# Reordering the last stage of a gated cross-attention and mixture-of-experts kernel: the last expert's down product, the routed rows' additions, and the last store

## The chip, the cores and the metric

One core of one Trainium2 chip runs the whole kernel. The metric is device time in microseconds of one execution, as a median of runs. Five engines matter: PE (TensorE, matrix products), DVE (VectorE), ACT (ScalarE), POOL (GpSimd) and SP (SyncE, which here only issues DMAs). PEld is the weight load that goes with each matmul.

## The reference

Four batches of 512 tokens with 512 features pass two layers. The first, per batch, is a quantised gated product with weights of its own. The second is a mixture of experts over all 2048 tokens, and the change lies in it:

```python
x = x + tanh(g_xattn[0]) * quantised_glu(layernorm(x), fside, ctx)
h = layernorm(x).reshape(-1, 512)                      # 2048 tokens
topk_w, topk_idx = top_k(softmax(h @ gate_w.T), 2)     # 16 experts, 2 per token
buf[e, pos] = h[token]                                 # 256 places per expert
expert_out = einsum(silu(buf @ w_gate) * (buf @ w_up), w_down)     # inner width 352
y = sum over the 2 experts of topk_w * expert_out[expert, pos]     # back to tokens
sh = (silu(h @ ws_gate) * (h @ ws_up)) @ ws_down       # shared expert, width 704
x = x + tanh(g_ffn[0]) * (y + sh)
```

All of it is float32.

## The kernel before

The residual `X` stays in SBUF as 16 tiles `X[:, j, :]` of 128 tokens by 512 features. Tiles 0 to 11 (batches 0 to 2) get their shared expert earlier; tiles 12 to 15 (batch 3) get it at the end of the kernel, after the routed experts.

*Routed experts.* A loop over `e` runs 16 experts of 256 token places, two halves `h` of 128. `gate_up(e)` computes the gate and up products (L1138) and writes the features to two tiles `home.h[h]` (named `h_e` in the profile; L1205 and L1213). `turn_features(e)` transposes both on TensorE (L1158, `tp_h`), six transposes. `join_features(e, h)` copies a transposed half from PSUM to `ehT` on VectorE (L1165). `down_routed(e)` makes the two down products into PSUM tiles `eo` (L974), of three chunks of the inner width each. `take_down(e, h)` copies one to SBUF on ScalarE (L1149) and stores it to the DRAM tensor `eo_dram` from ScalarE's own queue (L1150). The down product of an expert follows the gate and up product of the next one. For the last expert there is no next one: before the change, the gate product of chunk 0 of the shared expert stands between the turning of its features and its down.

*The end.* The shared expert of batch 3 has five full chunks of 128 of its inner width and a rest of 64. `chunk_steps(c)` gives for a chunk: four gate products (`pg`, L959), the silu on ScalarE (L963), four up products (`pu`, L959), and the product of both on VectorE (`times`, L966), which writes `hT`. The rest has one product `pr` for gate and up together (L998), its silu (L1002) and two products on VectorE (L1010). Then, for tiles `t` = 0 to 3 in two pairs `u`, `tokens_product` (L1024) and `rest_tokens` (L1030) multiply `hT` by the down weights into PSUM `sh`, and `tokens_add` (L1034) adds it to `X` and calls `store`, a DMA issued by SP (L1635).

*Routed rows.* `gather_result` (L1659) gathers on POOL, for one tile and one of its two experts, 128 rows of `eo_dram` by `slot` into a tile `yk`; there are 32 gathers and 20 buffers, and a gather beyond the 20th is issued after the addition that frees its buffer. `add_results(upto)` (L1670) adds rows to `X` on VectorE until `upto` of the 32 are done, in the order tiles 12 to 15, then 0 to 11, two rows a tile; the second addition of a tile below 12 is followed by its store. The gathers begin after `routed.close()`, which gives back the buffers of the routed experts, of which the buffers `yk` take the place.

*Order.* Everything here stands under `tc.manual_schedule()`: each engine runs its instructions in the order in which the program text emits them, and semaphores put the engines in step. The order of the last stage is written out by hand, and the tuples in the text say how far `add_results` goes at each place. PSUM has rings of buffers: `ps_t` (2, transposes), `ps_c` (2, down products) and `ps_mm` (4, tag `mm`: gate, up, rest and token products, taken in turn).

Of the kernel before, what the change touches and what calls it, by code (L numbers as in the profile page):

```python
# [9 lines left out]
F32 = mybir.dt.float32  # L10
# [5 lines left out]
ALU = mybir.AluOpType  # L16
# [4 lines left out]
P = 128  # L21
B, S, H = 4, 512, 512
HC = H // P
TT = S // P
NT = B * TT
# [3 lines left out]
E = 16  # L29
CAP = 256  # L30
# [6 lines left out]
CHUNKS_I = [(0, 128), (128, 128), (256, 96)]  # L37
CHUNKS_IS = [(c * P, min(P, IS - c * P)) for c in range((IS + P - 1) // P)]
FULL = IS // P
# [81 lines left out]
def flamingo_gated_kernel(  # L121
# [16 lines left out]
    nc = tc.nc  # L138
    vec, act, pe, pool = nc.vector, nc.scalar, nc.tensor, nc.gpsimd
# [5 lines left out]
    ps_c = ctx.enter_context(tc.tile_pool(name="ps_c", bufs=2, space=PSUM))  # L145
# [13 lines left out]
    X = const.tile([P, NT, H], F32, tag="X", name="X")  # L159
    x_flat = x.rearrange("b (t p) h -> p (b t) h", p=P)  # L160
    out_flat = out.rearrange("b (t p) h -> p (b t) h", p=P)
# [53 lines left out]
    tg_f = const.tile([P, 1], F32, tag="tg_f", name="tg_f")  # L215
# [756 lines left out]
    def down(acc, hT, t, wd, chunks):  # L972
        for c, (_, m) in enumerate(chunks):
            pe.matmul(  # L974
                acc, lhsT=hT[:m, c, bass.ts(t, P)], rhs=wd[:m, c, :], start=(c == 0), stop=(c == len(chunks) - 1)
            )

    def shared(b, done=None):
        s = SimpleNamespace()

        def chunk_steps(c, home=(shp, 2)):
            if c == 0:
                s.hT = shp.tile([P, len(CHUNKS_IS), S], F32, tag="hT", name="hT")
            return glu_steps(xTs[b], c * P, s.hT[:, c, :], home)

        def chunk(c):
            gate, silu, up, times = chunk_steps(c)
            for step in gate + up:
                step()
            silu()  # L990
            times()

        def rest_product(k):


            if k == 0:
                s.pr = ps_mm.tile([P, H], F32, tag="mm", name="pr")
            pe.matmul(s.pr, lhsT=wsr[:, k, :], rhs=xTs[b][:, k, :], start=(k == 0), stop=(k == HC - 1))  # L998

        def rest_silu():  # L1000
            s.g = shp.tile([P, S], F32, tag="g", name="g_rest", bufs=2)
            act.activation(s.g[:REST], s.pr[:REST], AF.Silu)  # L1002

        def rest_times(odd):

            gate, up, dst = (
                a.rearrange("p (u v q) -> p u v q", v=2, q=P)[:, :, odd]
                for a in (s.g[:REST], s.pr[REST:], s.hT[REST * odd : REST * (odd + 1), FULL, :])
            )
            vec.tensor_tensor(dst, gate, up, ALU.mult)  # L1010

        def rest():
            for k in range(HC):
                rest_product(k)
            rest_silu()
            rest_times(0)
            rest_times(1)

        accs = {}

        def tokens_product(t, c, last):
            if c == 0:
                accs[t] = ps_mm.tile([P, H], F32, tag="mm", name="sh")
            pe.matmul(accs[t], lhsT=s.hT[:, c, bass.ts(t, P)], rhs=wsd[:, c, :], start=(c == 0), stop=(c == last))  # L1024

        def rest_tokens(u, last):

            for odd in range(2):
                t, rows = 2 * u + odd, slice(REST * odd, REST * (odd + 1))
                pe.matmul(accs[t], lhsT=s.hT[rows, FULL, bass.ts(t, P)], rhs=wsd[rows, FULL, :], start=False, stop=last)  # L1030

        def tokens_add(t):
            j = b * TT + t
            vec.scalar_tensor_tensor(X[:, j, :], accs[t], tg_f, X[:, j, :], ALU.mult, ALU.add)  # L1034
            if done is not None:
                done(j)

        s.__dict__.update({k: f for k, f in locals().items() if callable(f)})

        s.chunk_steps = chunk_steps  # L1040
        s.all = [lambda c=c: chunk(c) for c in range(FULL)] + [rest]
        return s
# [7 lines left out]
    R = [SimpleNamespace(xg={}) for _ in range(E)]  # L1050
    HALF = HC // 2

    E_W = {e: {} for e in range(E)}
# [93 lines left out]
    def take_down(e, h):  # L1147
        eo = qb.tile([P, H], F32, tag="h", name="eo_sb", bufs=3)
        act.copy(eo, R[e].acc[h])  # L1149
        nc.scalar.dma_start(out=eo_dram[e * CAP + h * P : e * CAP + (h + 1) * P, :], in_=eo)  # L1150

    def turn_features(e):
        r = R[e]
        r.tps = []
        for h in range(CAP // P):
            tp = ps_t.tile([P, HC, P], F32, tag="tp", name="tp_h")
            for c in range(len(CHUNKS_I)):
                pe.transpose(tp[:, c, :], home.h[h][:, bass.ts(c, P)], ident)  # L1158
            r.tps.append(tp)

    def join_features(e, h):
        r = R[e]
        if h == 0:
            r.hT = qb.tile([P, len(CHUNKS_I), CAP], F32, tag="wc", name="ehT", bufs=2)
        vec.tensor_copy(r.hT[:, :, bass.ts(h, P)], r.tps[h][:, : len(CHUNKS_I), :])  # L1165

    def gate_up(e):
# [46 lines left out]
        if more:  # L1214
            for step in combine_tokens(e + 1):
                step()

    def down_routed(e):
        r = R[e]
        r.acc = {}  # L1220
        for h in range(CAP // P):
            r.acc[h] = ps_c.tile([P, H], F32, tag="c", name="eo")
            down(r.acc[h], r.hT, h, E_W[e]["down"], CHUNKS_I)
        take_down(e, 0)
        if e + 2 < E:
            load_down(e + 2)
# [392 lines left out]
    with tc.manual_schedule():  # L1619
        plan.run()  # L1620
        open_features()
        for e in range(E):
            gate_up(e)
            if e > 0:
                down_routed(e - 1)
            turn_features(e)
            if e == 1:
                routing_weights(qb)

    def store(j):
        nc.sync.dma_start(out=out_flat[:, j, :], in_=X[:, j, :])  # L1635

    sh3 = shared(B - 1, store)

    tiles = list(range(NT - TT, NT)) + list(range(NT - TT))
    with tc.manual_schedule():  # L1640
        chunks = [sh3.chunk_steps(0)]
        take_down(E - 2, 1)
        for step in chunks[0][0] + [chunks[0][1]]:
            step()
        for h in range(CAP // P):
            join_features(E - 1, h)
        down_routed(E - 1)
        take_down(E - 1, 1)
        for step in chunks[0][2] + [chunks[0][3]]:
            step()  # L1650
        routed.close()
        homes = 20
        results = ctx.enter_context(tc.tile_pool(name="results", bufs=homes))
        yks = []

        def gather_result():
            i = len(yks)
            yk = results.tile([P, H], F32, tag="yk", name="yk")
            pool.indirect_dma_start(  # L1659
                out=yk,  # L1660
                out_offset=None,
                in_=eo_dram,
                in_offset=bass.IndirectOffsetOnAxis(ap=slot[i % 2][:, tiles[i // 2] : tiles[i // 2] + 1], axis=0),
            )
            yks.append(yk)

        def add_results(upto):
            while added[0] < upto:
                j, k = tiles[added[0] // 2], added[0] % 2
                vec.scalar_tensor_tensor(  # L1670
                    X[:, j, :], yks[added[0]], wk[k][:, j : j + 1], X[:, j, :], ALU.mult, ALU.add
                )
                if k == 1 and j < NT - TT:
                    store(j)
                added[0] += 1
                if len(yks) < 2 * NT:
                    gather_result()

        added = [0]
        for i in range(homes):  # L1680
            gather_result()
        for c in range(1, FULL):
            chunks.append(sh3.chunk_steps(c, (results, 4)))
            for step in chunks[c][0] + [chunks[c][1]]:
                step()
        for k in range(HC):
            sh3.rest_product(k)
        sh3.rest_silu()
        for c, upto in zip(range(1, FULL), (7, 9, 12, 15)):
            for step in chunks[c][2]:  # L1690
                step()
            add_results(upto)
            chunks[c][3]()
            if c == 2:
                sh3.rest_times(0)
                sh3.rest_times(1)

        for u, uptos in enumerate(((22, 23), (27, 2 * NT))):
            for t in (2 * u, 2 * u + 1):
                for c in range(FULL - 1):  # L1700
                    sh3.tokens_product(t, c, FULL - 1)
            sh3.rest_tokens(u, False)
            for t, upto in zip((2 * u, 2 * u + 1), uptos):
                sh3.tokens_product(t, FULL - 1, FULL - 1)
                add_results(upto)
                sh3.tokens_add(t)
# [41 lines left out]
```

## Time and profile before

| | |
|---|---|
| median of 3 runs | 585.71 us (585.59 to 585.83) |
| the profiled execution's own time | 585.57 us |
| its span | 583.5 us |
| PE busy | 529.3 us (91%) |
| DVE busy | 405.1 us (69%) |
| ACT busy | 228.9 us (39%) |
| POOL busy | 138.2 us (24%) |
| last stage, chunk 0 of the shared expert to the end | 513.1 to 583.5 us |

Times in the profile count from the start of the span. A row of the timeline gives start, length, engine, line, operation, output and inputs, count, and in brackets how long the engine had been idle and which work ended that. A row of the windows gives, for a stretch, the busy time and number of instructions of each engine, TensorE's granted clock (1.00 is full speed), the mean busy share of the 16 DMA engines and what they moved.

### The profile page before, as it was taken

How to read it: one execution, taken by the hardware profiler on the slowest of the kernel's cores; microseconds unless marked ns; L12 is line 12 of the kernel's file. 1: busy time of each engine (PE TensorE's matmuls, PEld its weight loads, DVE VectorE, ACT ScalarE, POOL GpSimd, SP SyncE). 2: the span in 40 equal slices, each digit the busy share in tenths (PEclk: the TensorE clock that was granted, in tenths of full speed). 3: DMA queues.
4: the chain of work that ended last, by engine and by line, in shares of the span. 5: the costliest groups of instructions: out<-in, count | busy, mean ns of one | idle time of the engine just before them, and what ended most of it. 6: DMA issues, size and time to landing. Idle time of an engine off the chain costs nothing.

```text
span 583.5 us, 5816 instructions
## 1 busy us (share of the span) xinstructions
PE 529.3 (91%) x1760; PEld 275.0 (47%) x1764; DVE 405.1 (69%) x926; ACT 228.9 (39%) x380; POOL 138.2 (24%) x152
## 2 busy tenths in 40 slices
PE   0375499999999999999989999999999999999994
PEld 0232345444444444454455555555555555544441
DVE  3878778998999898987278666666666666304474
ACT  3465366646824272050135434434435343211000
POOL 1212130344143421100310111111212110007770
PEclk9995699999999999999999999999999999999999
DMA  8971012011402365010587999999999995215695
GB/s 295 359 229 38 0 54 92 0 38 54 91 1 54 56 232 155 20 72 1 131 209 223 264 249 269 276 236 276 262 260 274 276 276 173 87 72 160 200 319 187
DMA packets 93774, 95.05 MB, mean 163 GB/s; under 512 B 51488, under 2 KB 69920, under 8 KB 93744
## 3 DMA queue, kind: packets, MB, share of 16 engines
q1 hardware_dynamic: 84016, 69.52, 44.5%
q0 software_dynamic: 5120, 16.78, 9.2%
q10 hardware_dynamic: 4608, 8.39, 3.8%
q8 instruction: 14, 0.23, 0.2%
q14 instruction: 16, 0.13, 0.1%
HBM read 66.36 MB, written 16.78 MB: 142 GB/s over the span
## 4 chain that ended last, share of the span: by engine, by line
PE 79%; DVE 4%; issue 2%; POOL 1%; ACT 0%; DVEq 0%; POOLq 0%
PE b L1138 22%; PE eo L974 14%; PE pu L959 11%; PE pg L959 11%; PE sh L1024 9%; PE pr L998 2%; PE tp_h L1158 2%; PE acc L565 2%; PE sh L1030 1%; PE rowb L304 1%; PE acc L713 1%; DVE amw_w L414 1%; PE tp_am L296 1%; PE tp_x L760 1%; PE tp_q L358 1%
## 5 line engine op out<-in xcount | busy, mean ns | idle before, releaser
L974 PE MATMUL eo<-wd,ehT 128*128 128x512 f32 (+1 forms) x192 | 85.1, 592 | 0.0
L1089 POOL DMA_INDIRECT xg<-xn_dram,slot_token x32 | 34.8, 1088 | 195.7 <-DMA xp<-xg 161.0
L959 PE MATMUL pg<-xT,wsg 128*128 128x512 f32 x160 | 75.7, 603 | 0.0
L959 PE MATMUL pu<-xT,wsu 128*128 128x512 f32 x160 | 74.0, 595 | 0.0
L1024 PE MATMUL sh<-wsd,hT 128*128 128x512 f32 x160 | 73.9, 597 | 0.0
L974 PEld LDWEIGHTS eo<-wd,ehT 128*128 128x128 f32 (+1 forms) x192 | 36.4, 190 | 42.1 <-issue 37.7
L351 ACT COPY xgT<-xp 128x1024 int16<-128x1024 int16 x31 | 39.5, 1339 | 26.4 <-DMA xp<-xg 26.3
L1187 DVE TENSOR_TENSOR p<-p,b 128x352 f32<-128x352 f32 x16 | 8.3, 521 | 58.8 <-PE b L1138 58.8
L1659 POOL DMA_INDIRECT yk<-eo_dram,slot x32 | 33.5, 1048 | 55.7 <-PE pu L959 46.3
L959 PEld LDWEIGHTS pu<-xT,wsu 128*128 128x128 f32 x160 | 29.3, 190 | 31.2 <-issue 31.1
L1024 PEld LDWEIGHTS sh<-wsd,hT 128*128 128x128 f32 x160 | 28.9, 190 | 31.4 <-issue 30.4
L959 PEld LDWEIGHTS pg<-xT,wsg 128*128 128x128 f32 x160 | 29.0, 193 | 30.3 <-issue 29.5
L1138 PE MATMUL b<-T,S 128*128 128x352 f32 x128 | 40.6, 460 | 0.7 <-DVE S L1129 0.7
L1138 PE MATMUL b<-wg,xgT 128*128 128x352 f32 x128 | 40.6, 460 | 0.0
L1138 PE MATMUL b<-wu,S 128*128 128x352 f32 x128 | 40.5, 459 | 0.0
L1149 ACT COPY eo_sb<-eo 128x512 f32<-128x512 f32 x32 | 18.7, 585 | 47.5 <-PE eo L974 43.5
L1138 PEld LDWEIGHTS b<-T,S 128*128 128x128 f32 x128 | 24.2, 190 | 14.5 <-issue 1.2
L1138 PEld LDWEIGHTS b<-wu,S 128*128 128x128 f32 x128 | 24.3, 190 | 13.5
L490 POOL TENSOR_TENSOR wi<-wi,s_row 128x512 f32<-128x512 f32 x15 | 18.6, 1274 | 46.8 <-ACT s_row L475 46.8
L966 DVE TENSOR_TENSOR hT<-g,pu 128x512 f32<-128x512 f32 x20 | 13.6, 682 | 22.6 <-PE pu L959 22.2
L963 ACT ACTIVATE g<-pg 128x512 f32<-128x512 f32 x20 | 11.9, 596 | 41.9 <-PE pg L959 35.6
L1670 DVE SCALAR_TENSOR_TENSOR X<-yk,wk,X 128x512 f32<-128x512 f32 x32 | 23.1, 748 | 7.4 <-DMA yk<-eo_dram,slot 7.1
(219 smaller groups left out, 857.5 us busy)
## 6 DMA issues: line engine op xcount, KB each, us to landing
wg<-in_L_ffn_w_gate_dram SPq DMA_DIRECT2D x16, 704.0 KB, 5.0
wu<-in_L_ffn_w_up_dram SPq DMA_DIRECT2D x16, 704.0 KB, 6.2
wd<-in_L_ffn_w_down_dram SPq DMA_DIRECT2D x16, 512.0 KB, 5.8
eo_dram<-eo_sb ACTq DMA_DIRECT2D x32, 256.0 KB, 4.7
X<-in_x_dram SPq DMA_DIRECT2D x16, 256.0 KB, 8.3
wi<-in_fside_BxS2xS_dram SPq DMA_DIRECT2D x4, 1024.0 KB, 7.1
xn_dram<-yp SPq DMA_DIRECT2D x16, 256.0 KB, 2.0
out_dram<-X SPq DMA_DIRECT2D x16, 256.0 KB, 4.2
```

The source lines that it names most:

```text
L351: return (vec.tensor_copy if on is vec else act.copy)(dst, src)
L490: on.tensor_tensor(w.wi[:, t, :], w.wi[:, t, :], v.s_row, ALU.mult)
L959: pe.matmul(v.ps[name], lhsT=w[:, k, o : o + P], rhs=xT[:, k, :], start=(k == 0), stop=(k == HC - 1))
L963: act.activation(v.g, v.ps["pg"], AF.Silu)
L966: vec.tensor_tensor(dst, v.g, v.ps["pu"], ALU.mult)
L974: pe.matmul(acc, lhsT=hT[:m, c, bass.ts(t, P)], rhs=wd[:m, c, :], start=(c == 0), stop=(c == len(chunks) - 1))
L1024: pe.matmul(accs[t], lhsT=s.hT[:, c, bass.ts(t, P)], rhs=wsd[:, c, :], start=(c == 0), stop=(c == last))
L1089: pool.indirect_dma_start(out=xg.rearrange("p l n -> p (l n)"), out_offset=None, in_=xn_dram, in_offset=bass.IndirectOffsetOnAxis(ap=slot_ ...
L1138: pe.matmul(ps[:, :I], lhsT=lhs[:, k, :], rhs=rhs[:, k, :], start=(first and k == 0), stop=(k == HALF - 1), skip_group_check=not first,)
L1149: act.copy(eo, R[e].acc[h])
L1659: pool.indirect_dma_start(out=yk, out_offset=None, in_=eo_dram, in_offset=bass.IndirectOffsetOnAxis(ap=slot[i % 2][:, tiles[i // 2] : tile ...
L1670: vec.scalar_tensor_tensor(X[:, j, :], yks[added[0]], wk[k][:, j : j + 1], X[:, j, :], ALU.mult, ALU.add)
```

## The change

Four edits, all in the last stage:

- `down_routed` is split into `down_tile(e, h)` for one half. The loop over experts ends with expert 14; expert 15's gate and up product is followed by the first half of expert 14's down, the turning of expert 15's features, the second half of 14's down, and then both halves of 15's down. All of chunk 0 of the shared expert comes after that.
- The places up to which rows are added change from 7, 9, 12, 15 (at the up products of chunks 1 to 4) to 12, 15, 18, 21.
- The places at the four token tiles change from 22, 23, 27, 32 to 28, 28, 32, 32.
- For the last tile, `tokens_add` works in two halves of 256 columns; the first is stored from SP's queue and the second from ScalarE's.

```diff
         def tokens_add(t):
             j = b * TT + t
-            vec.scalar_tensor_tensor(X[:, j, :], accs[t], tg_f, X[:, j, :], ALU.mult, ALU.add)
-            if done is not None:
-                done(j)
+            last = done is not None and t == TT - 1
+            for cs, on in ((slice(0, H // 2), nc.sync), (slice(H // 2, H), nc.scalar)) if last else ((slice(0, H), nc.sync),):
+                vec.scalar_tensor_tensor(X[:, j, cs], accs[t][:, cs], tg_f, X[:, j, cs], ALU.mult, ALU.add)
+                if done is not None:
+                    done(j, cs, on)
...
+    def down_tile(e, h):
+        r = R[e]
+        if h == 0:
+            r.acc = {}
+        r.acc[h] = ps_c.tile([P, H], F32, tag="c", name="eo")
+        down(r.acc[h], r.hT, h, E_W[e]["down"], CHUNKS_I)
+
     def down_routed(e):
-        r = R[e]
-        r.acc = {}
         for h in range(CAP // P):
-            r.acc[h] = ps_c.tile([P, H], F32, tag="c", name="eo")
-            down(r.acc[h], r.hT, h, E_W[e]["down"], CHUNKS_I)
+            down_tile(e, h)
         take_down(e, 0)
...
-        for e in range(E):
+        for e in range(E - 1):
             gate_up(e)
...
+        gate_up(E - 1)
+        down_tile(E - 2, 0)
+        turn_features(E - 1)
+        down_tile(E - 2, 1)
+        for h in range(CAP // P):
+            take_down(E - 2, h)
+            join_features(E - 1, h)
+        for h in range(CAP // P):
+            down_tile(E - 1, h)
+            take_down(E - 1, h)
...
-    def store(j):
-        nc.sync.dma_start(out=out_flat[:, j, :], in_=X[:, j, :])
+    def store(j, cs=slice(0, H), on=nc.sync):
+        on.dma_start(out=out_flat[:, j, cs], in_=X[:, j, cs])
...
         chunks = [sh3.chunk_steps(0)]
-        take_down(E - 2, 1)
-        for step in chunks[0][0] + [chunks[0][1]]:
-            step()
-        for h in range(CAP // P):
-            join_features(E - 1, h)
-        down_routed(E - 1)
-        take_down(E - 1, 1)
-        for step in chunks[0][2] + [chunks[0][3]]:
+        for step in chunks[0][0] + [chunks[0][1]] + chunks[0][2] + [chunks[0][3]]:
             step()
...
-        for c, upto in zip(range(1, FULL), (7, 9, 12, 15)):
+        for c, upto in zip(range(1, FULL), (12, 15, 18, 21)):
...
-        for u, uptos in enumerate(((22, 23), (27, 2 * NT))):
+        for u, uptos in enumerate(((28, 28), (2 * NT, 2 * NT))):
```

## The prediction

> **What bounds the kernel now.** I read the end of the span first, in four views: windows by stage, the chain of waits, the timeline of VectorE, and the gathers' own page. The windows (stretch, length, then busy time of each engine, granted clock, DMA share):
>
> ```profile
> core 0: us, PE busy (x) PEld busy (x) DVE busy (x) ACT busy (x) POOL busy (x), PEclk, DMA share, GB/s
> 507.00:513.10 6.10, 6.10 (x19) 2.96 (x19) 1.04 (x3) 1.39 (x3) 0.00 (x0) 1.00 0.11 43
> 513.10:516.60 3.50, 3.50 (x11) 1.65 (x10) 1.02 (x2) 0.25 (x1) 0.00 (x0) 1.00 0.20 75
> ...
> 556.10:564.20 8.10, 8.10 (x22) 3.19 (x20) 5.69 (x9) 0.00 (x0) 6.27 (x7) 1.00 0.95 311
> 564.20:575.17 10.97, 10.97 (x29) 4.66 (x28) 4.81 (x7) 0.00 (x0) 3.76 (x4) 1.00 0.78 275
> 575.17:580.17 5.00, 0.82 (x2) 0.00 (x0) 4.90 (x7) 0.00 (x0) 0.00 (x0) 1.00 0.42 157
> 580.17:583.50 3.33, 0.00 (x0) 0.00 (x0) 0.00 (x0) 0.00 (x0) 0.00 (x0) 0.58 0.42 157
> ```
>
> TensorE is busy without a gap at granted clock 1.00 until 575.2; after that its last two matmul instructions remain and VectorE works alone for five microseconds. The chain of waits names the same hand-over (start, length, what):
>
> ```profile
> 573.02 1.06 PE sh L1030 x4
> 574.08 1.07 PE sh L1024 x2
> ...
> 575.84 1.41 DVE X L1670 x2
> ```
>
> What VectorE does there, by its timeline:
>
> ```profile
> 565.33 0.75 DVE L1034 SCALAR_TENSOR_TENSOR X<-sh,tg_f,X 128x512 f32<-128x512 f32 x1 [3.28 <-PE sh L1024]
> ...
> 567.32 2.85 DVE L1670 SCALAR_TENSOR_TENSOR X<-yk,wk,X 128x512 f32<-128x512 f32 x4
> 575.17 0.75 DVE L1034 SCALAR_TENSOR_TENSOR X<-sh,tg_f,X 128x512 f32<-128x512 f32 x1 [5.00 <-PE sh L1024]
> 575.84 3.64 DVE L1670 SCALAR_TENSOR_TENSOR X<-yk,wk,X 128x512 f32<-128x512 f32 x5
> 579.40 0.74 DVE L1034 SCALAR_TENSOR_TENSOR X<-sh,tg_f,X 128x512 f32<-128x512 f32 x1
> ```
>
> Five routed-row additions (L1670) stand after the shared addition of tile 14 and hold back that of tile 15. VectorE had been idle 5.00 us just before. The wait is one of order, not of work, provided the five rows had landed. The gathers:
>
> ```profile
> L1659 POOL DMA_INDIRECT yk<-eo_dram,slot x32: 942/950/1421, 525.9 to 567.9; - x32
> ...
> DMA to landing us min/median/max: 3.4/3.9/6.0
> ```
>
> The 32nd gather starts at 567.86 and the DMA page of 568 to 584 gives it 5.4 us to landing: 573.3. So it was there before TensorE ended, and all 32 additions can be over by then.
>
> **The change, part by part.**
>
> *Down of expert 15 ahead of chunk 0.* No instruction is added. TensorE's order from 507.4 is now 6 down matmuls, 6 transposes, 6 down, then down 15 (12), pg (8), pu (8), in place of 12, 6, pg, 12, pu. By the chain these are 5.16 + 0.66 + 3.44 + 5.16 + 3.43 us in either order, so chunk 0 still ends at 525.4: no change, if nothing runs dry. What may: (a) The transposes now start near 510.0; they need the second `h_e`, done at 508.10 + 0.53 = 508.63. Slack 1.4. (b) Before, pg covered the two copies to `ehT` (L1165). They ended at 514.12, 1.55 after the first transpose at 512.57; now 511.55. Down 15 starts when the second down half ends, 513.4. Slack 1.85; without that cover, each microsecond of lateness is one of TensorE. (c) `ps_c` has two buffers: down 15's first half needs ACT's copy of down 14's first half, 510.2 + 0.59 = 510.8, against 513.4; its second half needs 514.2 against 516.0. (d) The four `eo_dram` stores stay on ACT's queue, 0.33 us of issue each, spaced 2.6 us; the last moves from 522.63 to about 519.4, and the silu of chunk 0 behind it is needed only at 525.4. SP has nothing here.
>
> The gathers on POOL wait for the last of these stores, or for chunk 0: the trace puts the first one's wait down to `PE pu L959`. It starts at 525.89, 0.4 us after pu's last matmul but 1.26 us after the store's landing (522.63 + 2.0). So I take pu, which doesn't move: 525.89. At the other end they start 3.4 us earlier. That would only add slack below.
>
> *Additions placed anew.* Still 32, of 0.75 us. Before, 7 / 9 / 12 / 15 were done by the products of chunks 1 to 4, then 22, 23, 27, 32; now 12 / 15 / 18 / 21, then 28, 28, 32, 32. VectorE is in order, so each product now queues behind more additions, which wait for gathers. POOL issues one each 1.25 us alone and 1.35 to 1.54 beside additions (its timeline, 529.6 to 539.7). Additions 0 to 6 ran at 529.29 to 537.79, 1.42 apart and 3.75 after their gather. So: addition 11 at 529.29 + 11 x 1.42 = 544.9, over at 545.7; chunk 1's product was released at 546.12, 0.4 later. Addition 14 (gather 544.67) lands at 548.4, or at 550.0 if it takes the 5.3 us that gathers took once stores ran (555 to 565): done 549.2 to 550.7; chunk 2's product and the two rest products (0.69 + 0.86) then end at 551.1 to 552.3. TensorE needs them at 542.41 + 3 x 3.43 = 552.7, since the ring of four `mm` banks gives pr's bank to pu of chunk 4. This is the tightest point: slack 0.4 to 1.6, and I cost it at nothing. Chunks 3 and 4 are needed at 558.7 and 564.2 and come by 556 and 559. Addition 27 (gather 562.38 + 5) ends at 568.2, so tiles 12 and 13 get their shared addition at 568 to 569.5 and not 565.3 to 567.4; no one waits for those banks. Additions 28 to 31 follow, the last when gather 31 has landed: 573.3, over at 574.05. Slack to 575.17: 1.1.
>
> SP's stores follow the additions: the first at about 543 in place of 551.94. Until 573 some 14 stores, in place of 11, share the DMA with the gathers, but in 540:550 its share was 0.69 to 0.71, room for about four. A gather later by up to 1.1 us costs nothing.
>
> Here a rule speaks against the change. Beside additions a gather took up to 1.42 us against 0.94. The Trainium skill (GPSIMD Engine Reference, Specifications) says GpSimd shares its SBUF interfaces with VectorE and contends with instructions that have two SBUF inputs; L1670 has two. By it, the five additions that ran after the last gather now all run beside one: 5 x 0.2 = 1.0 us later. By the row, POOL had 0.3 us between gathers and was beside additions for most of them already, so some of that only changes place. By the rule the last addition ends at 575.05, by the row at 574.05; both lie before 575.17, so the sum is the same, but the rule eats the slack, and I keep its end for the range.
>
> *The end.* TensorE's last two matmuls end at 574.01 + 1.98 = 575.99. Tile 14's addition runs 575.17 to 575.92, so tile 15's starts at 576.02. Unsplit it would end at 576.77 in place of 580.14: **-3.37 us**.
>
> *Last store in halves.* One addition of 0.75 becomes two of 256 columns. TENSOR_TENSOR rows give 0.42 (256) and 0.69 (512), so 0.27 less: 0.48 each, the second about 0.4 after the first; over at 576.02 + 0.40 + 0.48 = 576.9, **+0.1**. The store issued at 580.17 was followed by the end 3.33 later. The last two stores moved 512 KB in 1.6 us of DMA time, so half a store saves up to 0.4; and SP need not issue (0.33) both. A second rule weighs here: the Trainium skill (DMA: Bandwidth & Descriptors, Issuing engines are not separate DMA queues) says that two queues save only issue time, as all run on the same 16 engines. By the row alone -0.4; by the rule the halves interleave and, with tile 14's store from 575.95 still moving, 0. No half store is in the trace. ACT's 256 KB stores landed in 2.0 to 3.8 us, SP's at the end in 2.0: bounds -0.4 and +1.8, value **-0.2**, near the stores in an empty DMA, which is what they meet.
>
> **Sum.** -3.37 + 0.1 - 0.2 = -3.5. The profiled run took 585.57 us, 2.07 of it outside its 583.5 us span, and lies 0.14 below the median of 585.71. So span 580.0, profiled time 582.1, median **582.2**.
>
> **The rivals.**
> 1. *The gathers become the bound of the end.* The slack of 1.1 is less than a busy DMA can add (maximum 6.0 to landing) plus the contention above: last addition over at 575.7 to 576.7, then 0.7 for tile 14 and 0.9 for tile 15: 1 to 2 us given back, 583.2 to 584.2. For it: DMA share 0.95 at 556 to 570. Against: more bytes move early. Still faster.
> 2. *ACT's store lands late*: at the bound of +1.8, and with 0.8 of rival 1 or of a short stall of TensorE, 584.8: no measurable change (within 0.2%, about what a measurement of this kernel can tell, 1.2 us). Against: the DMA is almost empty after 573.
> 3. *Slower: the additions starve TensorE at pr's bank.* The rest products stand behind addition 14. If gathers 9 to 14 slow down through the early stores and contention, everything behind shifts one for one. It costs from 0.4 to 1.6 us of lateness on; the gain is gone at 5.0 and it is slower by over 0.2% from 6.2 (one at 8 gives 588.7). The pace would have to grow from 1.42 to 1.85 us a gather over 14. No row shows that; the slowest was 1.72 from issue to issue.
> 4. *Nothing moves*, if landed rows set the additions at 575.84: but those five waited for no DMA.
>
> **How the numbers follow.** Forecast 0.69 (own range 581.6 to 583.2), rival 1 0.17, rivals 2 and 4 0.07, rival 3 0.07. Faster 0.86, same 0.07, slower 0.07. Below: 0.2 more for the split at its best, 0.1 if the halves follow each other without loss, and up to 0.3 that the last store of before may have waited behind the one issued 0.66 us ahead of it: 581.6. Above: through rival 1 to 584.2.
>
> **What the changed profile would show.** Right: no L1670 after 575.2; tile 15's two 256-column additions at about 576.0 and 576.4; the span's end 3.1 to 3.3 us after the second. TensorE without a gap from 507 to 575. Gather 31 landed before 575. Wrong: idle time of PE before pu of chunk 4 or before down 15; a wait of L1034 on `yk`'s gather in the end; the ACT store landing over 3 us after issue.

## The result

| | before | changed |
|---|---|---|
| median of 6 runs | 585.64 us (584.87 to 585.83) | 581.25 us (580.99 to 581.89) |
| ratio | | 0.9931, interval 0.9921 to 0.9941 |
| profiled execution's own time | 585.57 us | 581.28 us |
| its span | 583.5 us | 579.6 us |
| outside the span | 2.07 us | 1.68 us |

The change makes the kernel 0.7% faster: 4.39 us between these medians. The forecast was 3.5 us and 582.2 us, with a range down to 581.6, so the measured time lies 0.35 us below the range. In a later set of runs, with 25 runs of the kernel before beside it, the difference was 4.0 us (c_after: 581.33 against 585.3).

**The profile after.** The windows, cut as for the kernel before, and at the new places in the last microseconds (stretch, length, busy time of each engine, granted clock, DMA share):

```profile
564.20:575.17 10.97, 10.97 (x28) 4.40 (x26) 4.74 (x8) 0.00 (x0) 0.27 (x1) 1.00 0.57 204
575.17:576.54 1.37, 0.45 (x2) 0.00 (x0) 1.26 (x3) 0.00 (x0) 0.00 (x0) 1.00 0.09 33
576.54:579.60 3.06, 0.00 (x0) 0.00 (x0) 0.00 (x0) 0.00 (x0) 0.00 (x0) 0.84 0.45 157
```

Before, VectorE worked alone from TensorE's last matmul at 575.99 to 580.14, 4.15 us; the five of the prediction's window still held 0.82 us of TensorE's work. Now it is 0.92 us, from 575.62 to 576.54. The chain (start, length, what) now leaves TensorE only at its last matmul:

```profile
499.81 7.40 PE b L1141 x25
507.20 2.58 PE eo L974 x6
509.78 0.66 PE tp_h L1161 x6
510.44 7.74 PE eo L974 x18
518.17 3.44 PE pg L959 x8
521.61 3.43 PE pu L959 x8
...
572.65 1.06 PE sh L1030 x4
573.71 1.93 PE sh L1024 x4
575.63 0.03 issue
575.66 0.49 DVE X L1037
```

The moved down stands there as forecast: 6, 6, 18, then chunk 0, with each piece beginning where the one before ends. Also to be read here: 499.81 + 7.40 = 507.21 is the end of the last gate-and-up product, ahead of every edit; in the profile before it was 499.88 + 7.69 = 507.57. VectorE's timeline at the end:

```profile
568.91 0.75 DVE L1682 SCALAR_TENSOR_TENSOR X<-yk,wk,X 128x512 f32<-128x512 f32 x1 [0.23 <-DMA yk<-eo_dram,slot]
574.80 1.74 DVE L1037 SCALAR_TENSOR_TENSOR X<-sh,tg_f,X 128x512 f32<-128x512 f32 x3 [5.14 <-PE sh L1024]
```

The last row is added by 569.66, 5.1 us before tile 14's shared addition. The latter and the two halves end at 576.54; 576.9 was forecast, on an axis that starts 0.37 later at the gate-and-up product's end.

The last store of expert outputs on ScalarE's queue, and the first and last gather on POOL:

```profile
518.83 0.33 ACTq L1153 DMA_DIRECT2D eo_dram<-eo_sb  x1
...
522.09 0.95 POOL L1671 DMA_INDIRECT yk<-eo_dram,slot  x1 [42.94 <-PE pg L959]
...
563.52 0.95 POOL L1671 DMA_INDIRECT yk<-eo_dram,slot  x1 [0.30 <-DVE X L1682]
```

The first gather is 3.8 us earlier, now put down to `PE pg`. It started 1.26 us after that store landed (issued 518.83, landed 2.0 later), the distance of before (524.63 to 525.89). Two profiles alone do not settle what it waits for: a product of chunk 0 ended 0.48 us ahead of the gather in both, `pu` before and `pg` now, as both come equally long after the last down. Over all 20 profiles of this case, though, the distance to the landing is 1.259 or 1.260 us, while that to the product varies from 0.469 to 0.482. The gather waits for the store, whose semaphore is among those it waits for.

### The profile page after: what moved, and what is told of

Read it like the earlier page. It is cut to its first block, busy times and chain, and to the rows that moved or that the text cites. A ratio compares the mean times of both kernels' runs of the same rounds, so it can differ in the third digit from the quotient of the medians.

```text
span 579.6 us, 5820 instructions
## 1 busy us (share of the span) xinstructions
PE 527.3 (91%) x1760; PEld 274.4 (47%) x1764; DVE 406.3 (70%) x927; ACT 228.6 (39%) x380; POOL 137.7 (24%) x152
## 4 chain that ended last, share of the span: by engine, by line
PE 80%; DVE 4%; issue 2%; POOL 1%; ACT 0%; DVEq 0%; POOLq 0%
PE b L1141 22%; PE eo L974 14%; PE pu L959 11%; PE pg L959 11%; PE sh L1024 9%; PE pr L998 2%; PE tp_h L1161 2%; PE acc L565 2%; PE sh L1030 1%; PE rowb L304 1%; PE acc L713 1%; DVE amw_w L414 1%; PE tp_am L296 1%; PE tp_x L760 1%; PE tp_q L358 1%
## 5 line engine op out<-in xcount | busy, mean ns | idle before, releaser
L351 ACT COPY xgT<-xp 128x1024 int16<-128x1024 int16 x31 | 39.5, 1338 | 25.3 <-DMA xp<-xg 25.3
L1141 PEld LDWEIGHTS b<-wg,xgT 128*128 128x128 f32 x128 | 23.1, 190 | 10.9 <-issue 0.8
```

What stands on the lines that cost most here:

```text
L351: return (vec.tensor_copy if on is vec else act.copy)(dst, src)
L1141: pe.matmul(ps[:, :I], lhsT=lhs[:, k, :], rhs=rhs[:, k, :], start=(first and k == 0), stop=(k == HALF - 1), skip_group_check=not first,)
```

## The experiments

Since the starts of these executions differ, I measure the edited stage from the end of the last gate-and-up product (G, from the chain) to the end of the span, and set what lies outside the span beside it. Both are from the profiled execution; the medians and ratios are from all timed runs. G is a sum of two rounded rows, good to 0.01 us; "G to the end" goes to the trace's own end of span (583.49 before, 579.56 changed). "Outside" is taken from spans on record, which are rounded to 0.1 us, and so is good to 0.05.

| kernel | median us | ratio to before | G | G to the end | outside |
|---|---|---|---|---|---|
| before, on record | 585.64 | | 507.58 | 75.91 | 2.07 |
| c_before | 585.76 | 1.0004 (0.9996 to 1.0012) | 506.95 | 75.90 | 2.03 |
| only_split | 585.18 | 0.9999 (0.9990 to 1.0007) | 506.45 | 75.92 | 1.69 |
| only_down_again | 585.27 | 0.9999 (0.9990 to 1.0007) | 507.61 | 75.90 | 2.09 |
| only_adds | 582.27 | 0.9950 (0.9935 to 0.9964) | 507.01 | 72.54 | 2.13 |
| no_split | 582.52 | 0.9946 (0.9933 to 0.9960) | 508.16 | 72.53 | 2.07 |
| no_down | 581.62 | 0.9937 (0.9923 to 0.9951) | 507.48 | 72.35 | 1.75 |
| changed, on record | 581.25 | 0.9931 (0.9921 to 0.9941) | 507.21 | 72.35 | 1.68 |
| c_after | 581.33 | 0.9934 (0.9921 to 0.9948) | 507.21 | 72.35 | 1.68 |

**Both kernels again** (c_before, c_after; no edit).

> The kernel before, unchanged, as a control. Theory A (the excess over the forecast lies outside the edited stage and is a spread between executions): spans of single executions differ by 0.3 to 0.8 us, the last gate-and-up product ends between 507.2 and 507.6 us, and what lies outside the span is between 1.7 and 2.1 us, with 2.07 at the upper end. Theory B (the change itself shortens the stages ahead of it or the part outside the span): here the last gate-and-up product always ends near 507.57 and 2.07 us lie outside every span.

> The changed kernel, unchanged, as a control. From the last gate-and-up product's end to the end of the span: 72.4 us both theories (579.6 less 507.2). Theory A: that product's end lies between 507.2 and 507.6 and the part outside the span spreads from 1.7 us upward. Theory B: 507.2 and 1.7 us again.

The stage from G to the end repeats to 0.01 us. G does not: 506.45 to 508.16 over the kernels of the table, with nothing edited ahead of it. So the 0.37 us that the changed kernel gained before G is a spread of executions: Theory A holds there. What differed upstream can be followed through the four profiles of the two kernels (start times in us):

| event | before | c_before | changed | c_after |
|---|---|---|---|---|
| first instruction on the loaded `wi` (ScalarE, L410) | 10.25 | 10.19 | 9.70 | 10.16 |
| a VectorE instruction on `bn` (L289) | 61.56 | 61.50 | 61.01 | 61.47 |
| a product on VectorE into `hT` (L966) | 90.50 | 90.15 | 89.95 | 90.40 |
| ScalarE's copy `yp` (L351), after waiting for a store | 224.57 | 223.96 | 224.21 | 224.22 |
| G | 507.58 | 506.95 | 507.21 | 507.21 |

From 40 to 80 us the granted clock (the last column but two) is below full speed. Up to 60 us it is 0.74 and 0.58 before, 0.81 and 0.67 in the changed kernel, and the 0.55 us between them are the same in the first row as in the second. Windows of before between the second and the third row:

```profile
60.00:70.00 10.00, 4.00 (x19) 3.58 (x20) 8.71 (x21) 2.17 (x5) 1.09 (x1) 0.59 0.00 0
70.00:80.00 10.00, 9.19 (x30) 4.47 (x29) 6.92 (x18) 6.73 (x15) 0.09 (x1) 0.90 0.00 0
```

and of the changed kernel:

```profile
60.00:70.00 10.00, 4.55 (x21) 3.92 (x21) 8.20 (x20) 2.71 (x6) 0.54 (x1) 0.50 0.00 0
70.00:80.00 10.00, 8.45 (x29) 3.96 (x28) 7.47 (x19) 6.73 (x14) 0.64 (x1) 1.00 0.00 0
```

The changed kernel's 0.37 us came from the first load, which let it start 0.55 earlier. It was still 0.55 earlier at 90 us, so the clock gave nothing on balance: it averages 0.745 and 0.75 over these 20 us. ScalarE's wait for the store took back 0.19. In c_before the clock averaged 0.83 over the same stretch (0.66 and 1.00), and there 0.29 us were gained, and 0.26 more at the store. What lies outside the span, though, is not a spread: 2.03 to 2.13 in all 13 runs of c_before, 1.68 to 1.78 in all 5 of c_after. There Theory B holds.

**Each part alone, and each left out.** The last store whole (no_split), only the halves (only_split):

```diff
-            last = done is not None and t == TT - 1
+            last = False
```

> The change with the last tile's addition and store left whole, on SP's queue. By the prediction's steps: the addition starts at the same time after the last product and ends 0.13 us sooner than the second half did, the store takes 0.2 us more (0.4 by the trace's DMA rate, 0 if two halves only interleave): 0.1 us slower than the change (0 to 0.3), 3.4 us faster than before. A rival, that the second queue itself pays, expects over 0.5 us.

> The kernel before with only the last store in halves on two queues. Five row additions still stand ahead of the last tile's addition, so the end moves only by the split: 0.1 us faster than before (0 to 0.3). If the split carries the excess over the forecast, 0.8 us or more.

Inside the span the halves give 72.53 - 72.35 = 0.18 us on top of the change, and nothing alone: in only_split, close behind other stores, each half landed 2.0 us after issue, as whole stores do, and not 1.8. Outside it they give 0.4 us in both. From VectorE's end to the span's end it takes 3.02 us with halves (576.54 to 579.56) and 3.33 whole (577.36 to 580.69), so the smaller store saves 0.31 and costs 0.13 on VectorE.

Only the down moved (the tuples of before, last store whole), and everything but it (before with the new tuples and the halves):

> Only the down of expert 15 moved, once more, on a chip where the gathers land as in the profile of before. Same time as before within 0.3 us; 75.9 us from the last gate-and-up product to the end. Rival (earlier gathers shorten the end): 72.5.

> The kernel before with the additions placed anew and the last store in halves, but expert 15's down still around chunk 0's products, so that the gathers start about 3.4 us later. By the prediction's steps the last gather then lands 1.1 us before tile 14's addition and all else is in time: the same time as the change, within 0.3 us. Rival: the additions starve pr's bank or the last gathers bind the end: 1 to 2 us slower than the change, with a wait of the row additions on their gathers after 574 or idle time of TensorE before the up product of chunk 4.

The down alone is worth nothing: 75.90 again, though its first gather started at 522.49. VectorE's timeline of only_down_again shows why, the five additions still stand between the last two tiles:

```profile
575.21 0.75 DVE L1037 SCALAR_TENSOR_TENSOR X<-sh,tg_f,X 128x512 f32<-128x512 f32 x1 [5.00 <-PE sh L1024]
575.88 3.64 DVE L1682 SCALAR_TENSOR_TENSOR X<-yk,wk,X 128x512 f32<-128x512 f32 x5
579.43 0.75 DVE L1037 SCALAR_TENSOR_TENSOR X<-sh,tg_f,X 128x512 f32<-128x512 f32 x1
```

And without it the change is worth as much: 72.35. But how near no_down is to its limits can be read in the same view:

```profile
550.49 0.68 DVE L966 TENSOR_TENSOR hT<-g,pu 128x512 f32<-128x512 f32 x1
551.21 0.86 DVE L1010 TENSOR_TENSOR hT<-g_rest,pr 64x256 f32<-64x256 f32 x2
...
574.17 0.75 DVE L1673 SCALAR_TENSOR_TENSOR X<-yk,wk,X 128x512 f32<-128x512 f32 x1 [0.90 <-DMA yk<-eo_dram,slot]
575.07 1.73 DVE L1037 SCALAR_TENSOR_TENSOR X<-sh,tg_f,X 128x512 f32<-128x512 f32 x3
```

The rest products end at 552.07. The weight load that needs their bank started at 552.19, so 0.12 us were left. TensorE's weight loads do name this wait, but it is no delay: it is one of 40 equal gaps of 0.2 us, and the other 39 name no engine (view of waits, two rows: time in total, times, longest):

```profile
PEld pu L959 <- issue: 9.3, 39, 0.2
...
PEld pu L959 <- DVE hT L1010: 0.2, 1, 0.2
```

The last row is added by 574.92, 0.15 us before tile 14's addition starts. So the earlier down buys slack (5.1 us at the end in place of almost none), not time. An earlier run of the down alone (only_down) stood on a chip where the kernels ran some 10 us longer: 595.99 us against 595.22 for the kernel before, ratio 1.0038 (1.0017 to 1.0060). With runs of the kernel before from 586.40 to 600.31 us there, nothing is read from that difference; the four kernels timed on that chip (only_down, quarters, earlier_split, last_product_halves) are read only for what does not depend on it.

Only the additions:

> Only the additions placed anew; the down of expert 15 around chunk 0 and the last store whole, as before. By the prediction's main term, 3.37 us come from this alone: 72.5 from the last gate-and-up product to the end, 2.07 us outside the span, 582.0 to 582.6 us. Rival (late gathers bind without the earlier down): 73.5 or more.

```profile
571.19 2.98 DVE L1670 SCALAR_TENSOR_TENSOR X<-yk,wk,X 128x512 f32<-128x512 f32 x4
574.61 1.61 DVE L1034 SCALAR_TENSOR_TENSOR X<-sh,tg_f,X 128x512 f32<-128x512 f32 x2 [0.44 <-PE sh L1024]
```

The last four rows are added 0.44 us before tile 14's addition, and the two shared additions now follow each other. 75.91 - 72.54 = 3.37 us, the main term of the prediction to the hundredth, and 582.27 us.

**What shortens the part outside the span?** Edits of the loop `for cs, on in ...` of the changed kernel: both halves on SP, the whole store on ScalarE's queue, the queues swapped, four quarters, and the halves at tile 14 or tile 12 in place of tile 15.

```diff
-((slice(0, H // 2), nc.sync), (slice(H // 2, H), nc.scalar)) if last
+((slice(0, H // 2), nc.sync), (slice(H // 2, H), nc.sync)) if last      # both_on_sp
+((slice(0, H), nc.scalar),) if last                                     # whole_on_act
+((slice(0, H // 2), nc.scalar), (slice(H // 2, H), nc.sync)) if last    # halves_swapped
+[(slice(i * P, (i + 1) * P), (nc.sync, nc.scalar)[i % 2]) for i in range(4)] if last   # quarters
-            last = done is not None and t == TT - 1
+            last = done is not None and t == TT - 2                     # earlier_split
+            last = done is not None and t == 0                          # tile12_split
```

> The change with both halves of the last store on SP's queue. Asked: what shortened the part outside the span, 2.07 us in every run with the store whole on SP and 1.69 in every run with halves on two queues. Theory Q (a store on ScalarE's queue is in the end's way to be closed sooner): 2.07. Theory H (what matters is the size of the store that lands last): 1.69. Inside the span, from the end of the last gate-and-up product to the end: 72.4 as with two queues (0 to 0.2 more, as SP issues one store at a time, 0.33 us).

> The change with the last tile's addition whole and its store whole on ScalarE's queue. Theory Q: 1.69 us outside the span. Theory H: 2.07. Inside the span: 72.5, as without the split on SP.

> The change with the first half of the last store on ScalarE's queue and the second on SP's. Theory Q in its narrow form (the queue of the very last store decides): 2.07 us outside the span; in its wide form (any late store on ScalarE's queue): 1.69. Theory H: 1.69. Inside the span: 72.4.

> The change with the last tile's addition and store in four quarters of 128 columns, alternating between SP's and ScalarE's queues. Theory H (the part outside the span follows the size of the store that lands last): under 1.69 us outside, about 1.5. Rival N (what counts is only that the last store isn't whole): 1.69 again. Inside the span: four additions of about 0.35 at a pitch of 0.26 end 0.1 us later than the two halves, the last store saves 0.1: 72.4 from the last gate-and-up product to the end.

> The change with tile 14's addition and store in halves on two queues and the last tile's whole on SP's. Theory H: 2.07 us outside the span, as the last store is whole. Rival C (the number of stores, or any store on ScalarE's queue near the end, decides): 1.69. Inside the span: 72.5 to 72.6.

> The change with the halves at tile 12, whose shared addition is the first of the four and 10 us ahead of the end, and the last tile whole. On the part outside the span. If a store in halves on both queues anywhere at the end of the program shortens it (rival C): 1.7 us. If it must be one of the last two stores: 2.07.

| kernel | outside the span, all runs | G to the end |
|---|---|---|
| no_split: 16 stores on SP | 2.07 to 2.12 | 72.53 |
| whole_on_act: 15 on SP, 1 on ACT | 2.05 to 2.08 | 72.57 |
| both_on_sp: 17 on SP | 1.89 to 1.95 | 72.39 |
| halves_swapped: 16 on SP, 1 on ACT | 1.71 to 1.78 | 72.36 |
| earlier_split: 16 on SP, 1 on ACT | 1.69 to 1.77 | not comparable |
| tile12_split: 16 on SP, 1 on ACT | 1.68 to 1.73 | 72.48 |
| quarters: 17 on SP, 2 on ACT | 1.83 to 1.95 | not comparable |

The size of the last store (H) is refuted: with tile 12 in halves, 10 us before the end, and the last store whole, it is 1.7. ScalarE's queue as such (Q) is refuted by whole_on_act. It is a steady property of each program. In these seven it goes with how many stores there are on which queue, but in no order that I could find a rule for, and each edit also changes the program's instructions, which no run here separates from it. Why 16 and 1 are shortest stays open; no view of the profile shows this time. Inside the span the queue of the halves makes no difference over 0.04 us (72.35, 72.39, 72.36).

**What bounds the end now?** Three attempts at a better version: the last product of the last tile in two column halves (last_product_halves), all of the last tile's products in halves in two banks (last_tile_two_banks), and tile 14 finished before tile 15 (tile14_first), the last also with two banks.

```diff
+            for cs in (slice(0, H // 2), slice(H // 2, H)):          # last_product_halves: c == last of the last tile
+                pe.matmul(accs[t][:, cs], ..., rhs=wsd[:, c, cs], start=False, stop=cs.stop == H)
...
+                accs[t] = [ps_mm.tile([P, H], F32, tag="mm", name="sh") for _ in range(2)]   # two banks
...
+            early = FULL - 1 if u == 0 else 1                        # tile14_first
+            for c in range(early):
+                sh3.tokens_product(t + 1, c, FULL - 1)
             sh3.rest_tokens(u, False)
+            sh3.tokens_product(t, FULL - 1, FULL - 1)
+            add_results(upto)
+            sh3.tokens_add(t)
+            for c in range(early, FULL):
+                sh3.tokens_product(t + 1, c, FULL - 1)
+            sh3.tokens_add(t + 1)
```

> A step further than the change: the last product of the last tile in two column halves, so that its first half may be added while the second is made. Tile 14's addition holds VectorE until its next start, 0.67 us after 574.80 = 575.47; the first half then starts there and not at 575.66, the second 0.39 later, over at 576.34 in place of 576.54: 0.2 us faster than the change inside the span (72.2 from the last gate-and-up product). If the two more weight loads cost TensorE their 0.19 us each, nothing is left.

In that run the first half's addition began at 583.16, after the end of both half products (583.13), not between them, though VectorE was ready some 0.2 us sooner. Two regions of one PSUM tile gave no earlier start.

> A step further than the change: the last tile's products in two column halves in two PSUM banks, so that the first half's addition need not wait for the second half's product. Tile 14's addition holds VectorE until 0.67 us after its start (575.47 on the change's time axis), the first half starts there, the second 0.39 later: over at 576.34 in place of 576.54, 0.2 us less from the last gate-and-up product to the end (72.15). The last tile's matmuls double in number at half the columns; if each costs more than half, that gain is lost.

VectorE's end moved by 0.18 (G + 69.15 in place of G + 69.33), the end of the span not: 72.40. From VectorE's end it now took 3.25 us in place of 3.02. The DMA's row over the last 5.6 us of the changed kernel, 40 slices of 0.14 us, in tenths, shows tile 14's store and both halves as one block:

```profile
DMA  0000000000000000079999999997000000000000
```

That suggested that the three stores bind together, and the last two runs ask it.

> The change, with the last pair of tiles no longer finished side by side: TensorE makes all of tile 14's products (after one of tile 15's, which the rest products need), then the four left of tile 15's. Same matmuls, so TensorE ends at the same time; tile 14's addition and store move ahead by three products, 2.6 us. In the change the DMA moved tile 14's store and both halves, 0.52 MB, without a gap in the last stage; with tile 14's store gone before, the second half no longer waits: 0.3 us less from the last gate-and-up product to the end (72.05; bounds 72.35, if the landing alone binds, and 71.8).

> The same, with the last tile's products in two column halves in two PSUM banks. Now neither tile 14's addition nor its store stands ahead of the first half, which may start 0.43 us before TensorE's end; the second starts at that end and is over 0.5 us after it, in place of 0.88: with the emptier DMA 71.7 us from the last gate-and-up product to the end, 0.6 less than the change, some 580.7 us. If the DMA of the two halves binds instead, 72.05 as without the banks.

With tile 14's store gone early the same view shows the two halves alone (tile14_first):

```profile
DMA  9999820000000000000000599699400000000000
```

Yet G to the end is 72.32, no gain: the second half landed 1.8 us after issue in both. In the changed kernel the block was full but did not delay the last half. In last_tile_two_banks it did: there, closer behind tile 14's store, both halves landed 2.0 us after issue, and with tile 14's store gone (tile14_first_two_banks) in 1.7 and 1.8. ScalarE's half in the first and in the second (issue, size, us to landing):

```profile
out_dram<-X ACTq DMA_DIRECT2D x1, 128.0 KB, 2.0
...
out_dram<-X ACTq DMA_DIRECT2D x1, 128.0 KB, 1.8
```

So the two steps pay only together. Then VectorE ends 0.5 us after its last operand, at G + 68.96, and the span at G + 71.98, 0.37 less than the change. So the end is TensorE's last product, the addition behind it, and 3.0 us of store and closing. The median of tile14_first_two_banks is 581.16 us (ratio 0.9930, interval 0.9917 to 0.9944), not to be told from the change's 581.25 in so few runs.

## Why the prediction was right and wrong

- *The additions*: -3.37 forecast, 3.37 measured alone. Right, mechanism and size.
- *The halves*: +0.1 and -0.2 forecast, +0.13 and -0.31 measured. ScalarE's store landed in 1.8 us, less than the 2.0 to 3.8 us of the whole stores that it was bounded by. The rule that two queues save only issue time holds as far as the queues go (both_on_sp 72.39 against 72.35). The reading of it that the halves would save nothing did not hold: both halves on one queue save nearly as much (72.39 against 72.53 whole), so the saving came from the size, as the DMA rate suggested. Only in last_tile_two_banks did the stores hold each other up.
- *The down*: no gain, nothing dry. Right. But the gathers do not wait for chunk 0 as I chose; they started 3.4 us earlier, my other bound. The constant 1.26 us after landing was the better sign than the name in the brackets. The prediction counted on the late start; that the early one gave the change 5.1 us of slack was luck.
- *The slack*: with the late gathers (no_down) the rest products end at 552.07 (551.1 to 552.3 forecast), the last addition at 574.92 (574.05 by the row, 575.05 by the rule on shared interfaces). The deadline for the rest products was set too late, at 552.7: the weight load that waits for them starts at 552.19, so the slack was 0.12 and not 0.4 or more. From first to last gather it took 41.97 us before (41.97 and 41.99 in c_before and only_split), 42.70 in no_down and 43.43 in only_adds. Nearer to the rule's 1.0 us than to nothing, but these are single profiles, and the changed kernel alone took 41.43 and, in c_after, 42.15. The waits between gathers sum to 9.44 us in all of these, so only the gathers' own durations differ.
- *The sum*: -3.5 forecast, 75.91 - 72.35 = 3.56 measured from G. The step that failed is the last: "The profiled run took 585.57 us, 2.07 of it outside its 583.5 us span" was carried over unchanged, so a change of this part was put at nothing, without a reason. The edit of the store changed it to 1.68, by 0.4 us; why is open. And the base was one profiled execution, whose start alone is worth 0.37 us against the changed one's. With the spans unrounded, 2.08 and 1.72 us lie outside: 3.56 + 0.37 + 0.36 = 4.29, which is 585.57 - 581.28. The part outside alone would not have left the range: 585.71 - 3.56 - 0.36 = 581.8. It took the spread of executions as well, which is chance; c_after, 4.0 us below its own runs of the kernel before, shows little of it.
- *The range*: it went 0.6 us below the value, all for the last store and its split. It took in neither the spread of the starts nor a change outside the span. The three runs on which I leaned lay within 0.24 us; 25 later runs of the same kernel (c_after's) lay between 584.41 and 586.40.

## What to carry to other kernels

When an engine is idle for microseconds and then works off a queue in front of the last operation, look whether the queue's inputs had landed: then the order alone costs the time, and moving the work forward returns its length (3.37 us here for five additions, not the 5.00 us of idle time). Earlier inputs without that move returned nothing. The move without earlier inputs returned all of it, but with 0.15 to 0.44 us of slack at the end in place of 5.1: earlier inputs are a margin, not a gain. To compare a late edit, measure from the last unedited event, and let the range hold the spread of what lies ahead of it and outside the span.

## What was not expected of the hardware

The time outside the profile's span depends on the program, steadily: 2.03 to 2.13 us with all final stores whole, 1.68 to 1.78 with one of them in halves on two queues, even one 10 us from the end. Two executions of one kernel (before, c_before) stood 0.63 us apart ahead of the edits, of which 0.06 was there at the first load, 0.29 came in a stretch where the granted clock averaged 0.745 in one and 0.83 in the other, and 0.26 at a wait for a store. And a gather that waits for a store started 1.26 us after the store's landing in all 20 profiles, which the profile put down to whichever product had ended last.
